# First-step results split on VectorE between S's steps, and the last norm's statistics between later rounds of the search

## The chip, the core and the metric

The kernel runs on one core of a Trainium2 chip. The metric is the device time of one execution, in microseconds; the median of three executions of the kernel before is 3901.39 us.

## The reference

The graph has N = 2708 nodes with D = 512 features. Layer 0 is a graph attention layer with eight heads; layer 1, which the change touches, mixes three diffusions over two steps:

```python
S = S + jnp.eye(n)
Rf = S / jnp.clip(S.sum(axis=1, keepdims=True), 1e-12)
Rb = S / jnp.clip(S.sum(axis=0), 1e-12)[:, None]
Xf, Xb, Xa = (X, X, X)
Z = jnp.zeros_like(X)
for s in range(2):
    A = _adj_from_feats(Xa, W1, W2, W3)
    Xf = Rf @ Xf
    Xb = Rb @ Xb
    Xa = A @ Xa
    Z = Z + (Xf @ U1[s] + Xb @ U2[s] + Xa @ U3[s])
Y = X + Z
return (Y - Y.mean(-1)) / jnp.sqrt(Y.var(-1) + 1e-5) * gamma + beta
```

`_adj_from_feats` builds logits between all nodes, keeps of each row the largest softmax entries until 0.9 of the mass is reached, and takes the softmax over what is kept. Both layers are added to their input.

## The kernel before

The 2708 rows are 22 tiles of 128 (the last has 20). Layer 0 comes first and leaves `va_d` (the input of layer 1), a copy of it split into high and low parts (`vhl_d`), and S itself in memory (`s_d`). Then the second half runs, which the change is about.

**Rounds.** Each of the two steps handles the tiles in eleven pairs, one pair a round. In a round, VectorE searches the thresholds of the next pair (`search`), while TensorE uses the pair that has been found: `attended` transposes its kept weights (L1092), ScalarE copies the transposes out (`at`, L1096), and TensorE multiplies them with the values (L1111) in twelve chunks, six a tile. `mixed` then multiplies by U1, U2 and U3 (L1147). At a round's start TensorE makes the logits of the pair after next (L514), ScalarE copies them out (`p`, L516).

**The search.** `search` works in a first part (`rounds`: two rounds of the search in the first step and four in the second, each with two passes over the rows, L621), `choose`, and a last part, `finish`, which writes `keep` (L797 and after). Between `choose` and `finish` the function `late` is called: it records all of the round's work on TensorE, ScalarE and SP. On VectorE, what `late` records therefore stands between `choose` and `finish`. `keep` has two buffers, so `finish` waits until TensorE has transposed the pair before.

**Fills.** For the pair after next, ScalarE takes the exponentials and twelve looks (L546) over the logits, with thresholds `nth` (L566) that GpSimd works out from their sums in some ten small operations (L558 to L566). These are paced between the chunks of `attended`, so in ScalarE's order they stand between the `at` copies.

**S's products.** The products with S don't depend on the attention. The class `Products` cuts them into steps that are taken between the chunks as `others`. For each of six groups of up to four tiles (`quad`), 22 steps `product` (8 matmuls each, L982) make S times X, with operands `hl` and `s_r` that SP loads three deep (L972, L974). A step `scaled` then scales a tile on ScalarE by rows and by columns (`xe`, L989) and GpSimd's queue stores both to `xfb_d` (L990). The second step needs the products of these results, again as high and low parts: `split` loads a tile back on GpSimd's queue (L1019), splits it on GpSimd by four operations with 4097 (L1020 to L1023), and stores it to `fhl_d` or `bhl_d` (L1024). The buffers `split_hl` are two. In the steps `turned` (L999) TensorE uses these parts, and `stored` copies the results out (`xe`, L1005) and stores them to `xt_d` on GpSimd's queue (L1006). The first step takes 26 of these steps ahead of its rounds, 26 more in the round g = −1, and then 17 or 18 a round. `split(7)` is called at the start of the rounds after the first.

**The last norm.** In the second step, the finished rows `yo` of a round are normed in the next one. `normed` is called ahead of that round's search: statistics on VectorE (L143, L144), the inverse root on GpSimd (L145, L146), and a load of the residual on SP's queue (L1176). What it returns applies them (L1179, L1180) in the search's second round, `it == 1`.

**Order.** TensorE, ScalarE, VectorE and SP keep the order in which the program records their instructions; GpSimd's instructions are placed by the scheduler by its estimate of when each is ready. Every engine works through its own order and waits where it must. A DMA is issued in the order of the engine that issues it, and a DMA's wait holds up what that engine has behind it.

Of the kernel before, what the change touches and what calls it, by code (L numbers as in the profile page):

```python
# [9 lines left out]
F32 = mybir.dt.float32  # L10
BF16 = mybir.dt.bfloat16
I32 = mybir.dt.int32
# [3 lines left out]
OP = mybir.AluOpType  # L16
# [8 lines left out]
P = 128  # L25
# [28 lines left out]
def kernel(  # L54
# [19 lines left out]
    nc = tc.nc  # L74
    N, D = x.shape
# [6 lines left out]
    rows = [min(P, N - i * P) for i in range(NT)]  # L82
    cols = [slice(i * P, i * P + rows[i]) for i in range(NT)]
# [115 lines left out]
    with ExitStack() as l0:  # L199
# [13 lines left out]
        with tc.tile_pool(name="l0w", bufs=1) as wp, tc.tile_pool(name="l0p", bufs=2) as pp, \  # L213
# [376 lines left out]
    def search(lg, looked, early, late):  # L590

        (wide, small, _), grp, ps_, tot, thr, s = lg.pools, lg.grp, lg.p, lg.tot, lg.thr, lg.s
        v = nc.vector
        nx = NEXT[s]
# [53 lines left out]
        def rounds(n, aim_at=None):  # L650
            for it in range(n):
                v.tensor_tensor(d, ends[:, 1, 0:2], ends[:, 0, 0:2], op=OP.subtract)
                v.tensor_scalar(d[:, 1], d[:, 1], -1e-12, None, op0=OP.min)
                v.reciprocal(fr, d[:, 1])
                v.tensor_mul(fr, fr, ends[:, 0, 1])
                v.tensor_scalar(fr, fr, -0.95, -0.05, op0=OP.max, op1=OP.min)
                v.tensor_mul(fr, fr, d[:, 0])
                v.tensor_tensor(cur[:, 0], ends[:, 0, 0], fr, op=OP.subtract)
                v.tensor_mul(th, cur[:, 0], cur[:, 0])
                v.tensor_mul(th, th, th)  # L660
                if it in (aim_at or ()):
                    v.tensor_copy(fr, g0)
                    aim(g0, th)
                    v.tensor_tensor(fr, fr, g0, op=OP.subtract)
                    v.tensor_tensor(ends[:, :, 1], ends[:, :, 1], fr.unsqueeze(1).to_broadcast([P, 2, G]), op=OP.add)
                if it == 1 and begun:
                    begun.pop()()
                for i, pr in tiles:
                    mass(i, pr, th[:pr, i:i + 1], cur[:pr, 2, i:i + 1])
                v.tensor_tensor(fr, lg.top, cur[:, 2], op=OP.subtract)  # L670
                v.reciprocal(fr, fr)
                v.tensor_tensor(cur[:, 1], fr, g0, op=OP.subtract)
                v.scalar_tensor_tensor(side, cur[:, 1].unsqueeze(1).to_broadcast([P, 2, G]), 0.0, sides,
                                       op0=OP.is_ge, op1=OP.not_equal)
                v.copy_predicated(ends, side.unsqueeze(2).to_broadcast([P, 2, 3, G]),
                                  cur.unsqueeze(1).to_broadcast([P, 2, 3, G]))
                if it == 0 and aim_at is not None:
                    begun.append(early())

        begun = []  # L680
        rounds(ROUNDS[s], (0,) if s else ())
# [221 lines left out]
    with ExitStack() as st:  # L903
# [38 lines left out]
        class Products:  # L942
# [3 lines left out]


            def __init__(self):
                self.steps, self.ready, self.splits, self.split_at = [], {}, [], 0
# [35 lines left out]
            def scaled(self, t, j):  # L985
                pr = rows[t]
                for i, inv in enumerate((rinv, cinv)):
                    x = work.tile([P, D], F32, name="xe")
                    nc.scalar.activation(x[:pr], self.half[j][:pr], AF.Copy, scale=inv[:pr, t:t + 1])  # L989
                    nc.gpsimd.dma_start(out=xfb_d[i, cols[t], :], in_=x[:pr])  # L990
                    self.splits.append((i, t))

            def turned(self, quad, i, c):
                while (i, c) not in self.splits[:self.split_at]:
                    self.split(1)
                hl, s_r, w = self.operands((fhl_d, bhl_d)[i], quad, c)
                for k in range(KD):
                    for h in range(2):
                        nc.tensor.matmul(self.half[k][:, :w], lhsT=hl[:, h, k * P:(k + 1) * P], rhs=s_r[:, :w],  # L999
                                         start=(c == 0 and h == 0), stop=(c == NT - 1 and h == 1))  # L1000

            def stored(self, quad, q, i, k):
                w = len(quad) * P
                x = work.tile([P, D], F32, name="xe")
                nc.scalar.copy(x[:, :w], self.half[k][:, :w])  # L1005
                nc.gpsimd.dma_start(out=xt_d[q, i, :, k, :w], in_=x[:, :w])  # L1006

            def split(self, n):


                for i, t in self.splits[self.split_at:self.split_at + n]:
                    self.split_at += 1
                    pr = rows[t]
                    hl = parts.tile([P, 2, D], F32, name="split_hl")
                    x4 = parts.tile([P, D], F32, name="x4097", bufs=1)
                    if pr < P:
                        nc.gpsimd.memset(hl, 0.0)
                    high, x = hl[:pr, 0], hl[:pr, 1]
                    nc.gpsimd.dma_start(out=x, in_=xfb_d[i, cols[t], :])  # L1019
                    nc.gpsimd.tensor_scalar(x4[:pr], x, 4097.0, None, op0=OP.mult)  # L1020
                    nc.gpsimd.tensor_tensor(high, x4[:pr], x, op=OP.subtract)
                    nc.gpsimd.tensor_tensor(high, x4[:pr], high, op=OP.subtract)
                    nc.gpsimd.tensor_tensor(x, x, high, op=OP.subtract)  # L1023
                    nc.gpsimd.dma_start(out=(fhl_d, bhl_d)[i][t * P:(t + 1) * P], in_=hl)  # L1024

        S = Products()

# [143 lines left out]
        def normed(t, y):  # L1171

            pr = rows[t]
            mean, rs = moments(small, y[:pr], pr)
            xb = work.tile([P, D], F32, name="xw")
            nc.sync.dma_start(out=xb[:pr], in_=xb_d[cols[t], :])  # L1176

            def rest():
                nc.vector.scalar_tensor_tensor(y[:pr], y[:pr], mean, g_b[:pr], op0=OP.subtract, op1=OP.mult)  # L1179
                nc.vector.scalar_tensor_tensor(y[:pr], y[:pr], rs, xb[:pr], op0=OP.mult, op1=OP.add)  # L1180
                nc.gpsimd.dma_start(out=out[cols[t], :], in_=y[:pr])  # L1181

            return rest
# [61 lines left out]
        with tc.manual_schedule(engines={PE, ACT, DVE, SP}):  # L1245
            rest_of_first = []
            for s in range(STEPS):
# [37 lines left out]
                for g in range(-1, NP):  # L1285
# [4 lines left out]
                    if g + 3 < NP:  # L1290
                        lg.append(logits(g + 3))
                        lg[g + 3].queries()
                    if not s and g > 0:
                        S.split(7)
                    norms = [normed(t, y) for t, y in done] if s else []
                    done = []
                    if g < 0:
                        n = BEGUN - first if s else NT + 2 * G
# [60 lines left out]
                    if g + 1 < NP:  # L1359
                        ready = search(lg[g + 1], g >= 0, early, late)  # L1360
                    else:
                        if not s:

                            load_keys(1, 0, known * P)
                            ranks = Ranks()
                            others.insert(min(8, len(others)), lambda: ranks.sums(0, known))
                        for rest in norms:
                            rest()
                        late()
                        if not s:  # L1370
                            ranks.counted(0, known)
# [33 lines left out]
```

## Time and profile before

| | us |
|---|---|
| median of three runs | 3901.39 (3899.46 to 3902.29) |
| span of the profiled execution | 3908.7 |
| TensorE (PE) busy | 3388.9 (87%) |
| VectorE (DVE) busy | 2678.3 (69%) |
| ScalarE (ACT) busy | 1503.9 (38%) |
| GpSimd (POOL) busy | 1216.0 (31%) |
| first step's rounds, from the first transpose to the end of the last pair | 1302 to 2463 |
| second step's rounds, between the first and the last reciprocal of the kept mass that bound ten of them | 2710.8 to 3827.2 |

The profile is of one execution, taken with the hardware profiler. An engine is busy while it executes; waiting and issuing DMAs don't count, and TensorE's ends are modelled. A row of a group of instructions gives the line, the engine, the operation and its tiles, then the busy time and the mean duration, then the idle time of the engine before it and what ended that. "PE a L1111 <- ACT at L1096" in the view of waits says that the matmul of line 1111 waited for ScalarE's copy of line 1096. The clock is the share of TensorE's full clock that was granted.

### The profile page before, as it was taken

Reading aid. Unit: us, or ns where it says so; the run is one execution under the profiler, and the core shown is the slowest. Engines: PE = TensorE matmul, PEld = TensorE weight load, DVE = VectorE, ACT = ScalarE, POOL = GpSimd, SP = SyncE. Lnnn points to the kernel's source line nnn. Section 1 sums busy time; section 2 is a strip of 40 time slices with the busy share of each in tenths; the row PEclk is TensorE's granted clock in tenths of the full one; section 3 lists DMA queues with packets and bytes.
Section 4 is the critical chain, followed back from the end, with each engine's and each line's share of the span. In section 5 each row is a group of like instructions: output and inputs, shape, how many; then the busy total and the mean of one; then the engine's idle time right before and its main releaser. Section 6 shows DMA issues by size and latency. Waiting matters only on the chain. (4 is left out here: it accounts for less than half of the span.)

```text
span 3908.7 us, 35336 instructions
## 1 busy us (share of the span) xinstructions
PE 3388.9 (87%) x11058; PEld 1755.4 (45%) x11058; DVE 2678.3 (69%) x4727; ACT 1503.9 (38%) x2275; POOL 1216.0 (31%) x1447
## 2 busy tenths in 40 slices
PE   8998999999765596898789999976999699998787
PEld 4333333334444353554445555534555355554442
DVE  4687898899852443455544454369799978988992
ACT  2343211111124354544455661135555444545510
POOL 4115142243315717263641221122221232123211
PEclk9999999999878798999899999988999899999898
DMA  3475433323169555564554445565555355565441
GB/s 111 158 265 201 143 101 116 99 83 110 38 208 329 187 169 174 176 211 159 199 186 157 167 156 186 165 215 178 183 174 194 106 200 166 181 210 174 138 163 58
DMA packets 287348, 644.27 MB, mean 165 GB/s; under 512 B 37852, under 2 KB 86638, under 8 KB 284132
## 3 DMA queue, kind: packets, MB, share of 16 engines
q1 hardware_dynamic: 256488, 539.64, 42.3%
q0 software_dynamic: 30608, 101.84, 7.1%
q8 instruction: 89, 1.46, 0.2%
q14 instruction: 163, 1.34, 0.1%
HBM read 518.78 MB, written 122.57 MB: 164 GB/s over the span
## 5 line engine op out<-in xcount | busy, mean ns | idle before, releaser
L1111 PE MATMUL a<-va,at 128*128 128x512 f32 (+2 forms) x1936 | 910.6, 610 | 73.6 <-ACT at L1096 73.3
L426 PE MATMUL po<-e,fw 128*65 128x512 f32 (+4 forms) x2112 | 839.6, 553 | 33.7 <-DVE e L424 21.1
L424 DVE SCALAR_TENSOR_TENSOR e<-r_b,kk,a_c 128x512 f32<-128x512 f32 (+4 forms) x1056 | 752.2, 740 | 72.9 <-PE po L426 22.4
L546 ACT ACTIVATE junk_a<-p,nth 128x2708 uint8<-128x2708 f32 (+1 forms) x240 | 612.8, 2553 | 192.3 <-POOL nth L566 188.5
L999 PE MATMUL q<-s_r,hl 128*128 128x512 f32 (+1 forms) x2112 | 550.4, 409 | 75.3 <-ACT xe L1005 38.0
L1111 PEld LDWEIGHTS a<-va,at 128*128 128x128 f32 (+2 forms) x1936 | 344.5, 190 | 455.1 <-issue 354.3
L1147 PE MATMUL a<-u_k,v_t 128*128 128x512 f32 (+1 forms) x1056 | 491.2, 608 | 58.3 <-POOL v_t L1056 25.2
L426 PEld LDWEIGHTS po<-e,fw 128*65 128x65 f32 (+1 forms) x2112 | 287.1, 140 | 546.9 <-issue 269.5
L999 PEld LDWEIGHTS q<-s_r,hl 128*128 128x128 f32 x2112 | 381.3, 193 | 239.2 <-issue 92.6
L797 DVE SCALAR_TENSOR_TENSOR keep<-p,th 128x2708 f32<-128x2708 f32 (+1 forms) x44 | 134.5, 3056 | 466.0 <-PE t L1092 464.8
L621 DVE SCALAR_TENSOR_TENSOR junk<-p,th 128x2708 bf16<-128x2708 f32 (+1 forms) x132 | 414.6, 3141 | 4.0
L982 PE MATMUL q<-hl,s_r 128*128 128x512 f32 x968 | 275.8, 435 | 77.6 <-DMA s_r<-s_d 58.8
L1096 ACT COPY at<-t 128x512 f32<-128x512 f32 (+3 forms) x308 | 139.6, 474 | 496.1 <-PE t L1092 495.8
L1147 PEld LDWEIGHTS a<-u_k,v_t 128*128 128x128 f32 (+1 forms) x1056 | 191.1, 189 | 300.1 <-issue 206.2
L982 PEld LDWEIGHTS q<-hl,s_r 128*128 128x128 f32 x968 | 188.8, 199 | 158.6 <-issue 67.6
L514 PE MATMUL t<-keys,q_t 128*128 128x452 f32 x528 | 159.6, 426 | 97.0 <-ACT p L516 76.1
L799 DVE MAX8 vn<-keep 128x8 f32<-128x2708 f32 (+1 forms) x66 | 196.8, 2981 | 2.3
L541 DVE TENSOR_REDUCE nmx<-p 128x1 f32<-128x2708 f32 (+1 forms) x44 | 129.6, 2968 | 87.5 <-ACT p L516 87.4
L1056 POOL TENSOR_TENSOR v_t<-v_t,scales 128x1024 f32<-128x1024 f32 (+1 forms) x33 | 117.0, 3555 | 226.6 <-ACT v_t L1044 183.3
L1092 PE MATMUL t<-ident,keep 128*128 128x128 f32 (+1 forms) x968 | 148.3, 276 | 40.1 <-DVE keep L749 19.2
L516 ACT COPY p<-t 128x452 f32<-128x452 f32 (+2 forms) x264 | 130.9, 540 | 130.8 <-PE t L514 81.9
L408 ACT ACTIVATE s_c<-a_c 128x512 fp32r<-128x512 f32 (+3 forms) x132 | 76.2, 577 | 251.1 <-DMA a_c<-in_adj_t_dram 123.3
(313 smaller groups left out, 3536.4 us busy)
## 6 DMA issues: line engine op xcount, KB each, us to landing
s_r<-s_d SPq DMA_DIRECT2D x330, 256.0 KB
hl<-vhl_d SPq DMA_DIRECT2D x132, 512.0 KB
u_k<-in_L_gnn_U_dram SPq DMA_DIRECT2D x264, 256.0 KB
hl<-fhl_d SPq DMA_DIRECT2D x132, 512.0 KB
hl<-bhl_d SPq DMA_DIRECT2D x132, 512.0 KB
arow<-in_adj_dram SPq DMA_DIRECT2D x21, 1354.0 KB
s_d<-s_c SPq DMA_DIRECT2D x88, 256.0 KB
a_c<-in_adj_t_dram SPq DMA_DIRECT2D x84, 256.0 KB
```

The costliest lines, as they stand in the source:

```text
L424: nc.vector.scalar_tensor_tensor(e[:pr, :cw], r_b[:pr, i, :cw], kk[:pr, t, hd:hd + 1], a_c[t][:pr, :cw], op0=OP.max, op1=OP.mult)
L426: nc.tensor.matmul(po[i][:, :cw], lhsT=fw[:pr, t, hd, :], rhs=e[:pr, :cw], start=(t == 0), stop=(t == NT - 1))
L514: nc.tensor.matmul(pl[:, :c1 - c0], lhsT=q[:, i], rhs=self.keys[:, c0:c1], start=(i == 0), stop=(i == 1))
L546: nc.scalar.activation(junk[:pr], self.p[i][:pr], func, **kw)
L621: v.scalar_tensor_tensor(junk_b[:pr], ps_[i][:pr], th, ps_[i][:pr], op0=OP.is_ge, op1=OP.mult, accum_out=dst)
L799: v.max(vs, keep[i][:pr])
L982: nc.tensor.matmul(self.half[j], lhsT=s_r[:, j * P:(j + 1) * P], rhs=hl[:, h], start=(c == 0 and h == 0), stop=(c == NT - 1 and h == 1))
L999: nc.tensor.matmul(self.half[k][:, :w], lhsT=hl[:, h, k * P:(k + 1) * P], rhs=s_r[:, :w], start=(c == 0 and h == 0), stop=(c == NT - 1 and ...
L1092: nc.tensor.transpose(pt[:rows[c], j, :pr], keep[i][:pr, cols[c]], ident[:pr, :pr])
L1096: nc.scalar.copy(at[:r, j0:j1, :pr], pt[:r, j0:j1, :pr])
L1111: nc.tensor.matmul(pa[:pr], lhsT=at[:rows[c], j, :pr], rhs=va[:rows[c], c, :], start=(c == 0), stop=(c == NT - 1))
L1147: nc.tensor.matmul(pz[i][:rows[t]], lhsT=v_t[:, k, i * P:i * P + rows[t]], rhs=u_k, start=(n == 0 and k == 0), stop=(n == 2 and k == KD - 1))
```

## The change

Three parts of `Products` change. `split` no longer computes on GpSimd: it loads a tile on SP's queue, and at its next call masks the low bits away and subtracts on VectorE, and stores on GpSimd's queue. It is called one by one after S's steps 1 to 8 of each of the first step's rounds (`splitting`), instead of seven at a round's start. The stores of `scaled` and `stored` are issued by ScalarE. Besides, the last norm's statistics and its load are recorded in the search's third round, and their application in the fourth. All else is the same, TensorE's order too.

```diff
-                if it == 1 and begun:
-                    begun.pop()()
+                if it > 1 and begun:
+                    begun.pop(0)()
...
-                    begun.append(early())
+                    begun.extend(early())
...
-                    nc.gpsimd.dma_start(out=xfb_d[i, cols[t], :], in_=x[:pr])
+                    nc.scalar.dma_start(out=xfb_d[i, cols[t], :], in_=x[:pr])
...
-                nc.gpsimd.dma_start(out=xt_d[q, i, :, k, :w], in_=x[:, :w])
+                nc.scalar.dma_start(out=xt_d[q, i, :, k, :w], in_=x[:, :w])
...
-            def split(self, n):
+            def split(self):
...
-                for i, t in self.splits[self.split_at:self.split_at + n]:
+                for i, t, hl in self.taken:
+                    pr = rows[t]
+                    nc.vector.tensor_scalar(hl[:pr, 0].bitcast(I32), hl[:pr, 1].bitcast(I32), -4096, None,
+                                            op0=OP.bitwise_and)
+                    nc.vector.tensor_tensor(hl[:pr, 1], hl[:pr, 1], hl[:pr, 0], op=OP.subtract)
+                    nc.gpsimd.dma_start(out=(fhl_d, bhl_d)[i][t * P:(t + 1) * P], in_=hl)
                     self.split_at += 1
+                self.taken = []
+                if self.split_at < len(self.splits):
+                    i, t = self.splits[self.split_at]
                     pr = rows[t]
                     hl = parts.tile([P, 2, D], F32, name="split_hl")
-                    x4 = parts.tile([P, D], F32, name="x4097", bufs=1)
                     if pr < P:
                         nc.gpsimd.memset(hl, 0.0)
-                    high, x = hl[:pr, 0], hl[:pr, 1]
-                    nc.gpsimd.dma_start(out=x, in_=xfb_d[i, cols[t], :])
-                    nc.gpsimd.tensor_scalar(x4[:pr], x, 4097.0, None, op0=OP.mult)
-                    nc.gpsimd.tensor_tensor(high, x4[:pr], x, op=OP.subtract)
-                    nc.gpsimd.tensor_tensor(high, x4[:pr], high, op=OP.subtract)
-                    nc.gpsimd.tensor_tensor(x, x, high, op=OP.subtract)
-                    nc.gpsimd.dma_start(out=(fhl_d, bhl_d)[i][t * P:(t + 1) * P], in_=hl)
+                    nc.sync.dma_start(out=hl[:pr, 1], in_=xfb_d[i, cols[t], :])
+                    self.taken.append((i, t, hl))
...
+            def splitting(self, steps, n):
...
+                return [(lambda step=step: both(step)) if 0 < k < n else step for k, step in enumerate(steps)]
...
-                    if not s and g > 0:
-                        S.split(7)
-                    norms = [normed(t, y) for t, y in done] if s else []
+                    norms = done if s else []
...
-                    others = S.take(n)
+                    others = S.take(n) if s or g < 0 else S.splitting(S.take(n), 9)
...
-                        return lambda: [rest() for rest in norms]
+                        held = []
+                        return [lambda: held.extend(normed(*x) for x in norms), lambda: [rest() for rest in held]]
...
-                        for rest in norms:
+                        held = [normed(*x) for x in norms]
+                        for rest in held:
                             rest()
```

In VectorE's order the 44 splits stand between `choose` and `finish` of seven searches, by 7, 8, 8, 8, 7, 2 and 4. In SP's order each of the 44 loads stands behind the operands of the S step after which it is called. In GpSimd's order, in the first five of these rounds, the stores of five splits stand ahead of the operations that end in `nth`.

More of the change, by code (lines that the diff above doesn't have):

```diff
@@ L948, in __init__ @@
             def __init__(self):
-                self.steps, self.ready, self.splits, self.split_at = [], {}, [], 0
+                self.steps, self.ready, self.splits, self.split_at, self.taken = [], {}, [], 0, []
                 self.at = 0
@@ L994, in turned @@
                 while (i, c) not in self.splits[:self.split_at]:
-                    self.split(1)
+                    self.split()
                 hl, s_r, w = self.operands((fhl_d, bhl_d)[i], quad, c)
@@ L1005, in stored, with both @@
                 nc.scalar.copy(x[:, :w], self.half[k][:, :w])
-                nc.gpsimd.dma_start(out=xt_d[q, i, :, k, :w], in_=x[:, :w])
-            def split(self, n):
-                for i, t in self.splits[self.split_at:self.split_at + n]:
+                nc.scalar.dma_start(out=xt_d[q, i, :, k, :w], in_=x[:, :w])
[6 more added lines that the diff above has]
+                    nc.gpsimd.dma_start(out=(fhl_d, bhl_d)[i][t * P:(t + 1) * P], in_=hl)
                     self.split_at += 1
+                self.taken = []
+                if self.split_at < len(self.splits):
+                    i, t = self.splits[self.split_at]
                     pr = rows[t]
                     hl = parts.tile([P, 2, D], F32, name="split_hl")
-                    x4 = parts.tile([P, D], F32, name="x4097", bufs=1)
                     if pr < P:
                         nc.gpsimd.memset(hl, 0.0)
-                    high, x = hl[:pr, 0], hl[:pr, 1]
-                    nc.gpsimd.dma_start(out=x, in_=xfb_d[i, cols[t], :])
-                    nc.gpsimd.tensor_scalar(x4[:pr], x, 4097.0, None, op0=OP.mult)
-                    nc.gpsimd.tensor_tensor(high, x4[:pr], x, op=OP.subtract)
-                    nc.gpsimd.tensor_tensor(high, x4[:pr], high, op=OP.subtract)
-                    nc.gpsimd.tensor_tensor(x, x, high, op=OP.subtract)
-                    nc.gpsimd.dma_start(out=(fhl_d, bhl_d)[i][t * P:(t + 1) * P], in_=hl)
+                    nc.sync.dma_start(out=hl[:pr, 1], in_=xfb_d[i, cols[t], :])
+                    self.taken.append((i, t, hl))
+            def splitting(self, steps, n):
+                def both(step):
+                    step()
+                    self.split()
+                return [(lambda step=step: both(step)) if 0 < k < n else step for k, step in enumerate(steps)]
         S = Products()
```

## The prediction

> **What bounds the kernel now.** I read the page's engine shares first, then busy time by stretches of the first step's rounds, then who waited for whom inside them, then the timeline of single rounds. TensorE is busy 87% of the span, so the question is where its other 13% sits. The first step's rounds divide at 2055 us: the results of the first product are split into high and low parts on GpSimd until then, and no longer after it. The view by stretches (length, PE, PEld, DVE, ACT and POOL busy, clock, DMA share, GB/s):
>
> ```profile
> 1302.00:2055.00 753.00, 630.32 (x2072) 354.17 (x2072) 370.35 (x682) 369.24 (x460) 370.92 (x416) 0.92 0.53 180
> 2055.00:2463.00 408.00, 398.48 (x1378) 230.44 (x1378) 192.65 (x412) 185.20 (x236) 70.87 (x114) 1.00 0.51 168
> ```
>
> Six rounds with splits leave TensorE idle for 122.7 us and have POOL half busy; the nearly four rounds after leave 9.5 us. DVE and ACT have the same load per round in both. So POOL's work is the suspect. Who waited for whom, on TensorE between 1302 and 2055 us (total, times, longest):
>
> ```profile
> PE a L1111 <- ACT at L1096: 57.3, 14, 23.5
> PE a L1147 <- POOL v_t L1056: 25.2, 3, 18.1
> PE q L982 <- ACT xe L989: 18.7, 4, 9.1
> ```
>
> And on ScalarE between 1200 and 2055 us:
>
> ```profile
> ACT junk_a L546 <- POOL nth L566: 92.1, 7, 30.6
> ACT xe L989 <- DMA xfb_d<-xe: 42.9, 10, 11.1
> ```
>
> On TensorE after 2055 us the first row is 1.5 us and the two behind it are gone. The timeline shows the link: POOL works through split after split, and the thresholds `nth` come behind them.
>
> ```profile
> 1352.62 1.49 POOL L1020 TENSOR_SCALAR x<-split_hl 128x512 f32<-128x512 f32 x1 [2.31 <-DMA split_hl<-xfb_d]
> ...
> 1356.87 1.26 POOL L1023 TENSOR_TENSOR split_hl<-split_hl 128x512 f32<-128x512 f32 x1
> 1358.42 0.61 POOL L1024 DMA_DIRECT2D bhl_d<-split_hl  x1 [0.30 <-POOL split_hl L1023]
> 1359.07 0.74 POOL L559 TENSOR_TENSOR x<-half,powers 128x2 f32<-128x2 f32 x1
> ```
>
> The same moment on ScalarE:
>
> ```profile
> 1363.72 2.55 ACT L546 ACTIVATE junk_a<-p,nth 128x2708 uint8<-128x2708 f32 x1 [30.58 <-POOL nth L566]
> ```
>
> ScalarE's next `at` copy stands behind that look in its order, and TensorE waits 23.5 us for it at 1367.5. In the second step VectorE is the tighter engine: from 2710.8 to 3827.2 us (1116.4 us) it is busy 989.0, much as TensorE's 990.0. Its one avoidable wait there is for `yo`:
>
> ```profile
> DVE ln_st L143 <- POOL yo L1163: 93.3, 11, 64.2
> ```
>
> 64.2 us of it is the last norm of all, at the kernel's end; 26.4 us are in three rounds (13.1, 10.1, 3.2).
>
> **What the Trainium skill says.** "GPSIMD Engine Reference", section 4.1, sends elementwise work to VectorE, GpSimd being about twice as slow with two inputs; the trace agrees: POOL's four split operations take 1.49, 1.27, 1.27 and 1.27 us, VectorE's mask of the same shape (L178) 0.42. "VectorE: DVE Perf Modes", on the TRN2 errata, gives a float32 add of N elements (N+151)/0.96 ns, 0.69 us at 512; L239 shows 0.684. "DMA: Bandwidth & Descriptors", "Issuing engines are not separate DMA queues", says that issuing from another engine saves only issue time; so I book no bandwidth for it. "TensorE: Matmul & The Clock Gate", Part 1, ties the clock to how busy TensorE is; the stretches' 0.92 against 1.00 agree.
>
> **The change part by part.**
>
> *Splits leave POOL.* Removed per split: four operations, 1.87+1.56+1.27+1.40 = 6.1 us by their means, and a load issue of 0.59; 44 splits, 268+26 us. The stores of `xe` (92) leave POOL too, 51 us of issue. What this is worth is read from TensorE's idle time. If the six rounds were idle in the share of the rounds after (9.5 of 408), they would take 630.3/0.977 = 645 us: −108. A clock nearer 1.00 could make the busy time itself shorter: 304 ns a matmul record against 289, at most −31; the mix of matmuls differs, so I take −15. Before 1302, TensorE waits 22.2 us at 1293.7 for ScalarE, which had waited 24.4 us for `nth` and 11.1 for an `xfb` store; eight evacuations on two buffers stay there, some 9 us: −13.
>
> *Splits enter VectorE.* Two operations, 0.42+0.69 = 1.11 us, 44 times: 49 us, in seven rounds' `late`, ahead of `finish` in VectorE's order. There VectorE waits anyway for TensorE's transposes to free `keep`: 30 to 50 us in each of these rounds (41.6 until 1770.3, 49.5 until 1893.2). On the path: 0.
>
> *Loads enter SP's queue, two buffers.* This is the new wait. Load n needs the store of split n−2 landed, which needs VectorE to have come past its search; behind the waiting load stand the operands `hl` and `s_r` of S's next step, three deep, for which TensorE waits. I clock it from TensorE's first transpose of a round, called T. VectorE comes free at T+13 (2177 against 2164). Landing times by the DMA view, KB and us:
>
> ```profile
> vhl_d<-split_hl POOLq DMA_DIRECT2D x22, 512.0 KB, 2.9
> fhl_d<-split_hl POOLq DMA_DIRECT2D x22, 512.0 KB, 4.8
> ...
> split_hl<-xfb_d POOLq DMA_DIRECT2D x42, 256.0 KB, 3.5
> ```
>
> One turn of a buffer is 3.5 (load) + 1.1 (VectorE) + 0.6 (POOL's issue) + 4.8 = 10.0 us, two splits a turn. The split left over from the round before goes at T+13, is stored at T+19, and lets load 2 go; loads 4, 6 and 8 follow at about T+29, T+38 and T+48, the odd ones a microsecond behind. TensorE needs S's step k at T+4+5.9k while it does one a chunk (3.9 us of attention and 2 of S), and two in 7.5 us later: steps 7 and 9 at T+39 and T+49, whose operands land at T+41.5 and T+51. So some 5 us a round are lost in the five rounds that split seven or eight, +23; the ends are 0, where the store lands in 2.9 us as `vhl_d`'s does, and 12 a round, where it takes 3 us longer.
>
> *Stores of the splits stay on POOL.* In its order five stand ahead of the points of the pair after next. The fifth split is done at T+33, so `nth` comes at T+38 instead of T+29.6 (2193.5 in the round from 2163.9). ScalarE's look waits, and behind it the copy `at` that TensorE needs at T+41.6; look, `xa` and copy end at T+42: 1 to 3 us a round, +10 in all.
>
> *Stores issued by ScalarE.* 92 at some 0.4 us, as SP's rows have (0.32 to 0.43), behind ScalarE's own copy: 37 us on an engine that is idle 40 us and more a round. The waits for `xfb` and `xt` stores (42.9 and 11.0 us) shrink in return. ScalarE's copies are on TensorE's path, so this can be −10 to +15; I take 0.
>
> *Last norm.* The same 18 pairs of statistics and applications, two rounds of the search later; its loads don't move in SP's queue. VectorE starts a search 26.4 us earlier in all. At the third round, some 28 us after the search's start, `yo` (at most 13.1 after it) is there, so no wait follows. TensorE is nearly as full, so half is worth time: −13 (0 to −26).
>
> Sum: −108 −15 −13 +23 +10 −13 = −116. On the profiled span, 3908.7 to 3793. The timed runs have 3901.4 as median, 0.2% less; from there 3785.
>
> **Rivals.**
> 1. *The splits are freed but wait in line* (small gain). SP's loads are bound to VectorE and to landings, and turns of 13 us instead of 10 cost 12 us more a round, 60 more in all, with `nth` behind them 3 us a round later: about −40, 3860. For it: these are SP's first waits on VectorE in these rounds; against: SP's slack of three steps.
> 2. *Slower.* The same mechanism where it decides: the load at the head of SP's queue holds S's operands. The recovered idle time is 23 us a round in six rounds. It is lost from the point where VectorE comes free at T+31 rather than T+13, or a turn takes 15 us: four turns then end at T+73 against TensorE's T+49. A turn of 18 us would cost 36 us a round, 165 in 4.6 rounds, and ScalarE's copies behind `nth` another 40; against the 149 that the sum has without its new waits (116+23+10) that is +56, 3957. Against it: VectorE's T+13 holds in each round that TensorE bounds.
> 3. *It does not act.* If ScalarE's own load (59 us a round) rather than `nth` delayed `at`, only the waits for `xe` and `v_t` (49 us, half of it worth time) and for the norms go, −38, and +33 of new waits stand against them: 3896. Against it: after 2055 us ScalarE has the same load and TensorE waits 1.5 us.
>
> **How the numbers follow.** The forecast: 0.72, own range 3745 to 3830. Rival 1: 0.18. Rival 2: 0.06. Rival 3: 0.04. The best case, all idle time and clock recovered and no new wait, is −108−31−22−26 = −187, 3714. The range drops the ends of the first and all of rivals 2 and 3: 3735 to 3862. A measurement here can tell about 0.2% (8 us) from no change: faster 0.91, within it 0.03, slower 0.06.
>
> **What would show it.** Right: TensorE's waits for `at` between the first round and the end of the splits fall from 57 to under 25 us, the ones for `v_t` go; each of these rounds takes 104 to 112 us. SP shows waits of a `split_hl` load for VectorE or a store, and TensorE short waits for `s_r` behind them. VectorE's wait at L143 is left with the last one, of 64 us. Wrong: POOL's `nth` still late, now behind the stores; TensorE waiting over 10 us a round for `hl` or `s_r`; or VectorE's `keep` starting after TensorE's transposes.

## The result and the profile after

The changed kernel takes 3887.38 us (median of four executions, 3882.66 to 3888.83) against 3901.84 of the kernel before on the same chip: a ratio of 0.9958, 95% interval 0.9941 to 0.9975. That is 16 us faster. The prediction was 3785 us and its range ended at 3862, so the direction was right and the size was not.

The profiled executions (3908.7 us before, 3880.9 after) show that the change did two opposite things. Take as marks the starts of the rounds, the moment at which VectorE has the pair's `rden` (L898 before, L899 after). Lines from `split` on are 11 higher after: L1092, L1096, L1111, L1147 are now L1103, L1107, L1122, L1158.

| | before | after | difference |
|---|---|---|---|
| up to the first round of the second step | 2710.8 | 2632.1 | −78.7 |
| from there to the last round (second step) | 1116.4 | 1170.6 | +54.2 |
| last round and the norm at the end | 81.5 | 78.2 | −3.3 |

**The first step** went the way that the prediction described, for less: −78.7 us, where the terms of the splits in the prediction add to −103. The view by stretches (length; PE, PEld, DVE, ACT and POOL busy; clock, DMA share, GB/s) of the six rounds after the first, and of the second step, before:

```profile
1417.60:2144.50 726.90, 627.44 (x2068) 352.06 (x2066) 352.31 (x673) 369.55 (x460) 328.75 (x384) 0.94 0.54 180
...
2710.80:3827.20 1116.40, 990.01 (x3361) 562.21 (x3361) 989.00 (x1817) 538.47 (x644) 266.78 (x275) 0.95 0.50 167
```

and after:

```profile
1378.70:2062.70 684.00, 622.92 (x2067) 352.77 (x2065) 351.16 (x746) 372.30 (x460) 133.67 (x225) 0.97 0.59 201
...
2632.10:3802.70 1170.60, 1004.94 (x3361) 569.07 (x3361) 987.41 (x1817) 541.45 (x644) 307.42 (x241) 0.93 0.48 159
```

In the first row of each, POOL falls from 329 to 134 us and TensorE's idle time (length less PE busy) from 99.5 to 61.1 us. In the second row TensorE, VectorE and ScalarE have as many instructions as before, and yet the stretch is 54 us longer: 39 us of it are idle time of TensorE, 15 its busy time, at a clock of 0.93 instead of 0.95. GpSimd has fewer instructions, and is busy 41 us longer (the last section takes this up). Who waited for whom on TensorE in those six rounds, after:

```profile
PE a L1122 <- ACT at L1107: 17.1, 13, 5.1
PE q L983 <- DMA s_r<-s_d: 16.2, 11, 3.6
PE q L983 <- ACT xe L990: 9.3, 4, 6.2
```

The waits for `v_t` (25.2) are gone, those for `at` have halved from 33.8, and short ones for `s_r` are new: each what the prediction named. But the six rounds take 106 to 124 us each, where it had 104 to 112.

**The second step** holds what it did not name. Its waits after, as total, times and longest:

```profile
POOL ln_rs L145 <- DVE ln_mv L144: 145.2, 9, 30.3
...
POOL out_dram L1192 <- DVE yo L1191: 40.3, 18, 4.2
...
ACT junk_a L546 <- POOL nth L566: 135.0, 9, 23.6
...
PE a L1122 <- ACT at L1107: 51.5, 17, 17.5
...
DVE keep L798 <- PE t L1103: 61.7, 8, 15.2
```

Before, the same five were 36.6, 129.4, 73.4, 13.7 and 0.7 us. Read from the top it is a ring: GpSimd waits for VectorE's statistics, the thresholds `nth` come late, ScalarE's looks wait for them and its `at` copies behind the looks, TensorE waits for `at`, and VectorE waits for TensorE's transposes before it may write `keep`. The timeline of GpSimd in one round (start, duration; the idle time before and its end in brackets) shows the head of the ring:

```profile
3367.24 0.23 POOL L145 TENSOR_SCALAR ln_rs<-ln_mv 128x1 f32<-128x1 f32 x1 [17.69 <-DVE ln_mv L144]
3367.55 0.58 POOL L146 TENSOR_TENSOR ln_rs<-ln_rs,nhalf 128x1 f32<-128x1 f32 x1
3368.11 2.83 POOL L145 TENSOR_SCALAR ln_rs<-ln_mv 128x1 f32<-128x1 f32 x1
3371.03 3.35 POOL L146 TENSOR_TENSOR ln_rs<-ln_rs,nhalf 128x1 f32<-128x1 f32 x1
3374.35 0.70 POOL L559 TENSOR_TENSOR x<-half,powers 128x2 f32<-128x2 f32 x1
3378.56 0.67 POOL L1192 DMA_DIRECT2D out_dram<-yo  x1 [3.51 <-DVE yo L1191]
...
3391.55 0.25 POOL L566 TENSOR_SCALAR nth<-th_a 128x6 f32<-128x6 f32 x1
```

The norm's small operations (L145, L146) and its stores (L1192) are GpSimd's, and in GpSimd's order they stand ahead of the points of the pair after next, L558 to L566. `nth` is there 61.0 us after the round's start at 3330.8. The same in the kernel before, where the store waits for an application that VectorE makes in the search's second round; `nth` ends at 3429.9, 44.5 us after the round's start at 3385.4:

```profile
3413.58 0.64 POOL L1181 DMA_DIRECT2D out_dram<-yo  x1 [19.34 <-DVE yo L1180]
...
3419.91 1.46 POOL L558 TENSOR_TENSOR x<-tot,powers 128x2 f32<-128x2 f32 x1 [1.60 <-ACT p L553]
...
3426.89 3.04 POOL L566 TENSOR_SCALAR nth<-th_a 128x6 f32<-128x6 f32 x1
```

Here the store is not what comes last: behind it GpSimd still waits 1.60 us for the exponentials that ScalarE makes for the pair after next (L553). Over the second step before there are nine such waits, 15.6 us; after the change one is left, of 0.2 us. So before, the norm was done when the exponentials came; after, the exponentials are done when the norm comes.

ScalarE and TensorE at the end of the chain, after:

```profile
3391.83 2.55 ACT L546 ACTIVATE junk_a<-p,nth 128x2708 uint8<-128x2708 f32 x1 [19.01 <-POOL nth L566]
...
3397.67 2.93 PE L1122 MATMUL a<-va,at 128*128 128x512 f32 x3 [10.40 <-ACT at L1107]
```

### The profile page after: what moved, and what is told of

Same layout as the page of the kernel before. It is cut to its first block, busy times and chain, and to the rows that moved or that the text cites. A ratio compares the mean times of both kernels' runs of the same rounds, so it can differ in the third digit from the quotient of the medians.

```text
span 3880.9 us, 35319 instructions
## 1 busy us (share of the span) xinstructions
PE 3394.0 (87%) x11058; PEld 1755.9 (45%) x11058; DVE 2669.8 (69%) x4815; ACT 1511.9 (39%) x2275; POOL 929.9 (24%) x1135
## 5 line engine op out<-in xcount | busy, mean ns | idle before, releaser
L1122 PE MATMUL a<-va,at 128*128 128x512 f32 (+2 forms) x1936 | 910.9, 610 | 70.9 <-ACT at L1107 70.7
L1122 PEld LDWEIGHTS a<-va,at 128*128 128x128 f32 (+2 forms) x1936 | 345.2, 191 | 453.3 <-issue 353.4
L1158 PE MATMUL a<-u_k,v_t 128*128 128x512 f32 (+1 forms) x1056 | 487.3, 604 | 32.5 <-ACT xa L1130 18.7
L1107 ACT COPY at<-t 128x512 f32<-128x512 f32 (+3 forms) x308 | 140.4, 477 | 518.7 <-PE t L1103 513.0
L1158 PEld LDWEIGHTS a<-u_k,v_t 128*128 128x128 f32 (+1 forms) x1056 | 190.7, 188 | 270.5 <-issue 207.7
L1067 POOL TENSOR_TENSOR v_t<-v_t,scales 128x1024 f32<-128x1024 f32 (+1 forms) x33 | 98.0, 2982 | 425.2 <-ACT v_t L1055 343.4
L1103 PE MATMUL t<-ident,keep 128*128 128x128 f32 (+1 forms) x968 | 149.6, 277 | 28.5 <-DVEq L882 16.6
```

The lines of the kernel that those rows point to most:

```text
L1103: nc.tensor.transpose(pt[:rows[c], j, :pr], keep[i][:pr, cols[c]], ident[:pr, :pr])
L1107: nc.scalar.copy(at[:r, j0:j1, :pr], pt[:r, j0:j1, :pr])
L1122: nc.tensor.matmul(pa[:pr], lhsT=at[:rows[c], j, :pr], rhs=va[:rows[c], c, :], start=(c == 0), stop=(c == NT - 1))
L1158: nc.tensor.matmul(pz[i][:rows[t]], lhsT=v_t[:, k, i * P:i * P + rows[t]], rhs=u_k, start=(n == 0 and k == 0), stop=(n == 2 and k == KD - 1))
```

## The experiments

Theory A: the second step's loss comes from the norm, through GpSimd's order. Rival B: it comes from the stores that ScalarE now issues, or from a lower clock (0.93 against 0.95). Each ratio below is to the kernel before, with its 95% interval; microseconds from ratios are on 3902 us.

### The norm undone, and the norm alone

The changed kernel with the norm's part taken back, and the kernel before with that part alone:

```diff
-                if it > 1 and begun:
-                    begun.pop(0)()
+                if it == 1 and begun:
+                    begun.pop()()
...
-                    norms = done if s else []
+                    norms = [normed(t, y) for t, y in done] if s else []
```

> The changed kernel with only its norm part undone: the last norm's statistics stand again ahead of the search and the application in the search's second round; splits and stores stay as changed. Theory A (the second step's loss of 54 us comes from the norm: GpSimd waits for VectorE's later statistics and application with the thresholds of the pair after next behind it) expects about 3887-54 = 3833 us (3825 to 3845), the second step back at some 1116 us, ScalarE's wait for nth there near 73 us. Rival B (the loss comes from ScalarE issuing the xt stores, or from a lower clock) expects 3887 within 8 us, second step still near 1170 us.

> The kernel before with the norm part alone. Theory A expects it slower by the second step's loss less the few us won at the end: 3902+54-3 = about 3950 us (3935 to 3960), with GpSimd waiting at L145 some 145 us in all. Rival B expects no change, 3894 to 3905.

Undone: 3848.57 us, 0.9867 (0.9851 to 0.9884), so the norm's part costs the changed kernel 0.9958−0.9867, about 36 us. Alone: 3945.74 us, 1.0115 (1.0096 to 1.0134), 45 us slower than before. Theory A's direction holds twice and rival B's "no change" falls. The undone version misses A's 3825 to 3845 by 4 us: its second step is 1129.5 us, 13 longer than before, so not all of the 54 us is the norm's. That remainder stays in part open; the section on the stores has what is known of it. The lower clock comes with the norm's part: with that part alone, which leaves TensorE's order as it was, it falls to 0.93 too.

### One round sooner, off GpSimd's queue, and the store alone moved

Three versions of the changed kernel move the last thing that GpSimd waits for. The first runs both pieces one round of the search sooner:

```diff
-                if it > 1 and begun:
+                if it > 0 and begun:
```

The second takes the statistics ahead of the search again, and has the store of the output issued by SyncE, recorded behind the attention's operands; the third moves only the store:

```diff
-                nc.gpsimd.dma_start(out=out[cols[t], :], in_=y[:pr])
+                return lambda: nc.sync.dma_start(out=out[cols[t], :], in_=y[:pr])
...
                             xa, _ = attended(s, grp, keep, rden, fills, others, lambda: None)
+                            for store in stores:
+                                store()
```

> The changed kernel with the norm's two pieces one round of the search earlier each: statistics in the second round, application in the third. Theory A expects about half of the loss back, as GpSimd's wait shrinks by one round (some 9 us of 17 a pair): 3855 to 3872 us, GpSimd's wait at L145 at 50 to 80 us instead of 145. Rival B expects 3887 within 8 us.

> The changed kernel with the statistics ahead of the search again, the application left late (third round), and the store of the output issued by SyncE behind the attention's operands, so that nothing late of the norm is in GpSimd's queue. Theory A (it is the queue and not the lateness) expects the loss back and a little more, since the store no longer holds GpSimd either (19 us in one round of the kernel before): 3810 to 3835 us. If lateness itself costs (the buffer of yo, VectorE's order), it stays above 3865. Rival B expects 3887 within 8 us.

> The changed kernel with only the store of the output taken out of GpSimd's queue (SyncE issues it behind the attention's operands); statistics stay in the third round of the search. GpSimd waits 145 us at ln_rs and 42 us at the store in the changed kernel's second step. If ln_rs, which stands first, is what holds nth up, little comes back: 3875 to 3887. If the store is the one, 3840 to 3855.

They take 3845.65 us (0.9861, 0.9845 to 0.9878), 3842.46 us (0.9852, 0.9836 to 0.9868) and 3849.6 us (0.9854, 0.9836 to 0.9873): alike, and each some 40 us better than the changed kernel. Two expectations were off: one round sooner brings back all that undoing the norm does, not half of it, and off GpSimd's queue misses its 3810 to 3835 by 7 us, so that freeing GpSimd from the store won nothing further. Of the two cases set up for the store alone, the second came true, although GpSimd's longer wait is at L145. A long wait at L145 only says where GpSimd arrives first; `nth` follows the last thing that it waits for, and that was the store behind an application in the fourth round. With the store gone the last is the statistics in the third. The two versions whose last thing is in the third round also have the same waits. One round sooner:

```profile
ACT junk_a L546 <- POOL nth L566: 98.0, 9, 18.3
...
DVE keep L798 <- PE t L1103: 24.7, 7, 9.4
```

Only the store moved:

```profile
ACT junk_a L546 <- POOL nth L566: 99.9, 9, 18.3
...
DVE keep L798 <- PE t L1103: 24.8, 6, 10.7
```

So the norm's part is a trade on VectorE: it saves the waits for `yo` (28.9 us in the second step before) and pays with waits for `keep`. The search round of the norm's last thing ahead of `nth` sets ScalarE's wait for `nth`. VectorE's waits in the second step are given as a pair (for `keep` + for `yo`); the last row is the last version of the experiments:

| kernel | norm's last thing, search round | ScalarE's wait for `nth` | VectorE's waits | second step |
|---|---|---|---|---|
| before | application, 2nd | 73.4 | 0.7 + 28.9 | 1116.4 |
| norm alone | application, 4th | 134.2 | 63.2 + 0 | 1162.7 |
| norm undone | application, 2nd | 72.3 | 0.7 + 33.6 | 1129.5 |
| off GpSimd's queue | statistics, ahead | 77.6 | 2.0 + 38.1 | 1132.5 |
| one round sooner | application, 3rd | 98.0 | 24.7 + 0 | 1133.6 |
| only the store moved | statistics, 3rd | 99.9 | 24.8 + 0 | 1135.8 |
| changed | application, 4th | 135.0 | 61.7 + 0 | 1170.6 |
| last version below | statistics, 2nd | 74.4 | 13.2 + 0 | 1118.1 |

The first two rows have the splits and stores of the kernel before; the last has the stores on GpSimd and a third buffer for `xe`. The fourth round costs 46 us against the second on the kernel before, and 35 us or more against all others on the changed one. Between the third round and a norm ahead of the search the second step hardly differs (1132.5 to 1135.8): one wait takes the other's place.

### Stores issued by ScalarE

> The kernel before with only the stores of xe moved to ScalarE; splits and norm as before. If the splits themselves (6.1 us each) hold nth up, this wins little: 51 us of 345 us leave GpSimd and ScalarE waits less for xfb (47.5 us), 3880 to 3895. Rival: GpSimd's blocking on stores that wait for ScalarE (55.6 us at L990) is the main thing; then it wins most of the 55 us, 3845 to 3865.

> The kernel before with only the 44 xfb stores issued by ScalarE. Both kinds of stores together gave +15 us (+11 to +22). If it is the xfb stores (first step: the split's loads behind them wait up to 24.5 us on GpSimd, TensorE's first-round wait for s_r grows from 21.9 to 31.4), +8 to +15: 3910 to 3920. If it is the xt stores, 3898 to 3906.

> The kernel before with only the 48 xt stores issued by ScalarE. If the cost lies here (second step 1126 us instead of 1117), 3910 to 3918; else 3898 to 3906.

> The version with the norm off GpSimd's queue (3842 us), with the 92 stores of xe issued by GpSimd again. The prediction has their move at 0 (-10 to +15): 3842 within 8 us. Rival: the move is what costs the second step some 13 us there (ScalarE issues 44 xt stores among its copies), then this is faster, 3825 to 3835. Other rival: the stores behind other work on GpSimd make ScalarE wait for xe again (47.5 us before), then slower, 3855 or more.

The edit, whole and by halves, and the reverse of it on the version with the norm off GpSimd's queue:

```diff
-                    nc.gpsimd.dma_start(out=xfb_d[i, cols[t], :], in_=x[:pr])
+                    nc.scalar.dma_start(out=xfb_d[i, cols[t], :], in_=x[:pr])
...
-                nc.gpsimd.dma_start(out=xt_d[q, i, :, k, :w], in_=x[:, :w])
+                nc.scalar.dma_start(out=xt_d[q, i, :, k, :w], in_=x[:, :w])
```

Alone on the kernel before, ScalarE's stores cost time: 3918.25 us, 1.0043 (1.0029 to 1.0057), 17 us; both theories of that run, which had a gain, were wrong. By halves: the `xfb` stores do nothing, 1.0002 (0.999 to 1.0014); the `xt` stores cost 1.0024 (1.0011 to 1.0037), 9 us, and the second step, in which 32 of the 48 lie, takes 1132.9 us. The halves add to less than the whole, but the intervals allow it. Back on GpSimd in the version with the norm off its queue: 3838.82 us, 0.9832 (0.9819 to 0.9845), 8 us less than with ScalarE, but the two intervals overlap. So this part is a loss on the kernel before. How the `xt` stores cause it stays open: no wait of TensorE, ScalarE or VectorE in the second step is longer by more than 7 us than in the second profile of the kernel before (next run), but for one of 14.8 us for `yo` on ScalarE that another row has less of; VectorE's waits there grow by 6.5 (`rden`) and 4.5 us (`yo`), PE busy by 9.

> The kernel before once more, for a second profile: whether its second step takes 1116 us again (then the versions with the splits moved, 1130 us there, lose some 13 us to something that the change does) or some 1125 to 1130 us (then that difference is the spread between executions).

A second profile of the kernel before has its second step at 1117.7 us, and the version with only the `xfb` stores moved has 1117.6. So the 1126.3 us of all stores and the 1132.9 of the `xt` stores on ScalarE hardly come from the spread between executions alone, though with one profile each their size is uncertain. On the versions with the splits on VectorE the second step doesn't show it: with the norm off GpSimd's queue it takes 1132.5 us with the stores on ScalarE and 1133.4 with them back on GpSimd. The split part alone (next), stores on GpSimd, has 1124.8. So the 13 us left over above are not explained by the stores' issuer alone. With the norm's statistics and application moved so that no wait for `yo` is left, they go (1118.1 us, last version below).

### The splits alone, and without their loads and operations

> The kernel before with the split part alone: masks and differences on VectorE, loads on SyncE; stores of xe on GpSimd and norm as before. The prediction's terms for this part are -108-15-13+23+10 = -103, 3798. From the runs so far (-52 for splits and ScalarE's stores together, the stores +7 to +15 of it) it should give -60 to -67, 3835 to 3843. If the two parts need each other, less than that.

> The split part alone, without the split: no load of the results and no operation, only one load at the start, whose rows are stored 44 times in place of the high and low parts (so later products with them compute other values; the searches don't depend on them). SyncE, VectorE and the turn of two buffers are then out of it. The prediction's terms without its new waits are -108-15-13 = -136, which would be 3769. If the splits still cost what the prediction has for waits (33 us), this is 33 us faster than the split part alone (3835): about 3802. If the missing gain was never theirs (idle time on TensorE from p, xe and the first operands), 3820 to 3835, with TensorE still idle over 45 us in the six rounds after the first (69.6 in the split part alone).

The split part alone (stores and norm as before) takes 3834.78 us, 0.9821 (0.9807 to 0.9836): −70 us. It is the better part of the change by itself; with ScalarE's stores added it is the version with the norm undone (0.9867, +18 us), with the norm's part the changed kernel (0.9958, +36 us). The other run leaves the split out, and puts this in place of `split`'s body:

```diff
-                for i, t, hl in self.taken:
...
+                if self.split_at < len(self.splits):
+                    i, t = self.splits[self.split_at]
+                    if not self.taken:
+                        self.taken.append(parts.tile([P, 2, D], F32, name="split_hl"))
+                        nc.sync.dma_start(out=self.taken[0], in_=vhl_d[:P])
+                    nc.gpsimd.dma_start(out=(fhl_d, bhl_d)[i][t * P:(t + 1) * P], in_=self.taken[0])
+                    self.split_at += 1
```

It takes 3798.69 us, 0.9725 (0.9708 to 0.9741): −107 us, and by the ratios 37 less than the split part alone. As its stores wait for no result, GpSimd issues all 44 by 1339 us, in the first round, so the six rounds behind it have no split's load, operation or store. These six rounds, by the view of stretches:

```profile
1371.80:2024.60 652.80, 613.49 (x2070) 347.58 (x2068) 310.90 (x672) 369.06 (x460) 123.35 (x214) 0.98 0.50 168
```

and those of the split part alone, with TensorE's longest row of waits there:

```profile
1369.30:2064.40 695.10, 625.55 (x2067) 352.79 (x2065) 351.22 (x746) 370.16 (x460) 147.96 (x253) 0.96 0.58 198
```

```profile
PE q L983 <- DMA s_r<-s_d: 26.0, 9, 8.4
```

Without the split the row for `s_r` is gone and the waits for `at` hardly differ, 14.6 against 15.3 us. TensorE's idle time is 39.3 us instead of 69.6, its busy time 12 us less at a clock of 0.98 instead of 0.96. So the split on its new engines still costs some 37 us; in these rounds 26 are TensorE's waits for S's operands, 12 its busy time. As the run takes out the loads, VectorE's two operations and the stores' traffic together (the DMA share falls from 0.58 to 0.50), how much each has is not shown; the waits for `s_r` fit the loads in SyncE's queue. And 39 us of idle time are not the splits' at all: 14.6 for `at`, 11.6 for `xe`, 10.2 for `p` and the rest in crumbs.

### Loads on GpSimd, and a third buffer

Both on the version with the norm off GpSimd's queue (0.9852):

```diff
-                    nc.sync.dma_start(out=hl[:pr, 1], in_=xfb_d[i, cols[t], :])
+                    nc.gpsimd.dma_start(out=hl[:pr, 1], in_=xfb_d[i, cols[t], :])
```

> The version with the norm off GpSimd's queue (3842 us), with the loads of the splits issued by GpSimd instead of SyncE: nothing that waits for a split's store stands ahead of S's operands any more. If SyncE's wait for the two buffers costs what the prediction has (23 us; TensorE's waits for s_r there are 54.2, of which 28.0 is one at the first round's start), they fall to some 30 us and the time to about 3820 (3815 to 3832). Rival: the waits for s_r come from elsewhere (the operands' own landing, TensorE taking steps in twos) or move into GpSimd's queue ahead of nth; then the time stays within 8 us of 3842 or rises.

It changes nothing in all: 3850.95 us, 0.9855 (0.9841 to 0.9868). Inside, the wait has moved. TensorE, 1194 to 2060 us, loads on SyncE:

```profile
PE q L983 <- DMA s_r<-s_d: 54.2, 24, 28.0
...
PE a L1122 <- ACT at L1107: 18.5, 15, 5.5
```

and loads on GpSimd:

```profile
PE a L1122 <- ACT at L1107: 41.2, 16, 8.8
PE q L983 <- DMA s_r<-s_d: 40.1, 12, 30.3
```

The one long wait at the first round's start apart, `s_r` falls from 26 to 10 us, and `at` rises by 23, as now the points stand behind the split's loads: ScalarE's wait for `nth` in this stretch rises from 35.1 to 63.0 us. The load has to wait in somebody's queue, and both queues carry something TensorE needs.

```diff
-                    x = work.tile([P, D], F32, name="xe")
+                    x = work.tile([P, D], F32, name="xe", bufs=3)
```

> The version with the norm off GpSimd's queue (3842 us), with three buffers for xe instead of two. In the eight evacuations ahead of the first round ScalarE waits about 12.5 us for xfb stores and TensorE 19.2 us for the logits' copy behind them; with a third buffer that should fall by 4 to 8 us: 3832 to 3840. Rival: the round's start is set by something else (VectorE's thresholds), then no change.

3832.55 us, 0.9817 (0.9804 to 0.9831), by the ratios 14 us less, more than the 4 to 8 expected. ScalarE's wait for `xfb` stores falls from 20.2 to 10.3 us, TensorE's for the logits' copies at the first round from 19.2 to 15.8. These 3.4 us are all that the trace shows on TensorE; where the rest would come from is not shown.

### Versions that beat both kernels

> Splits on VectorE as changed, norm off GpSimd's queue, three buffers for xe, stores of xe on GpSimd. If the gains of the third buffer (-13 us against 3842) and of the stores left on GpSimd (-7) add, 3820 to 3830; if both are the same wait for a free xe, 3832 as with the third buffer alone.

> Splits on VectorE; xe stores on GpSimd, three xe buffers; the norm's statistics in the second round of the search, its application in the third, the store of the output on SyncE, so that the last thing GpSimd waits for ahead of the thresholds is in the second round, and VectorE no longer waits for yo (28.9 us in the second step of the kernel before). If VectorE's wait is worth half of its time there, as the prediction has it, some 13 us better than 3832: 3815 to 3825. If GpSimd's wait eats it, 3828 to 3836.

The first takes 3832.32 us, 0.9806 (0.9788 to 0.9825): the third buffer and GpSimd's stores don't add. The second changes only the norm against it: statistics in the search's second round, application in the third, the store on SyncE. It takes 3815.91 us, 0.9763 (0.9749 to 0.9778), 17 us less again and 76 less than the changed kernel by the ratios. In its second step VectorE's waits are the smallest of all (13.2 for `keep`, no row for `yo`), and the stretch is back at 1118.1 us, from 1130.1:

```profile
2615.70:3733.80 1118.10, 992.32 (x3361) 563.50 (x3361) 1000.52 (x1817) 539.22 (x644) 305.67 (x255) 0.95 0.50 166
```

## Why the prediction was wrong, by its own steps

**"Last norm", −13, "so no wait follows": the step that failed.** Measured +36 (+45 on the kernel before): of the 100 us between the predicted sum and the result, half. The step followed VectorE's queue and SyncE's. Of the moved code it counted the statistics, the applications and the loads; it left out what the same two functions issue on GpSimd, the small operations L145 and L146 and the two stores of the output, and so never asked what stands behind them. Behind them stands `nth`, the one thing that the first half of the prediction was about. The trace of before had a sign of it: GpSimd waited 19.34 us for VectorE's `yo` at the output's store, right ahead of L559, and its wait behind that for the exponentials was 1.60 us, which leaves some 2 us of room for a later norm (an estimate from this one round). What the step said of VectorE itself held: it no longer waits for `yo`. The saving itself was of the right size: where the norm's last thing ahead of `nth` stays in the second round, it is 17 us.

**"Splits leave POOL" −108, clock −15, before 1302 us −13: right mechanism, −107 measured for the three instead of −136.** That is the run without loads and operations. The term that was too large is −108: it took the idle share of the rounds after 2055 us (9.5 of 408 us) for all rounds. Those rounds have 1.5 us of waits for `at` and 3.3 for `xe`; the six rounds with splits keep 14.6 and 11.6 even when no split is computed. The first round's term was too large too: TensorE's wait for the logits' copies fell from 22.2 to 17.1 us in that run (19.9 in the changed kernel), not by 13. The clock's term held without the splits' waits (PE busy 613.5 against 627.4), not with them (622.9).

**"Loads enter SP's queue, two buffers" +23, "Stores of the splits stay on POOL" +10: +37 measured together.** The sum was nearly right, its division was not, and that is luck. `s_r` waits are 26.0 us in the split part alone, near the +23. `at` waits hardly differ with and without the split, so the +10 is not there; in its place TensorE's busy time is 12 us longer, at a lower clock.

**"Splits enter VectorE", 0 on the path: held.** The new subtraction took 0.693 us a time, as priced from the Trainium skill, "VectorE: DVE Perf Modes", TRN2 errata; the mask took 0.427, as the trace of before had it for L178. GpSimd's 1.27 us for an operation with two inputs are to be set beside these 0.693, not beside the mask as the prediction does: a factor of 1.8. VectorE is busy 351 us in the six rounds as before (352), which the prediction had not said: some 41 us of splits came in, and VectorE's other operations became 42 us shorter (see the last section).

**"Stores issued by ScalarE", 0 (−10 to +15): +17 and +18 measured.** That is just past the bad end of its bounds; taking the stores back on another version won 8 us, with overlapping intervals. ScalarE's 42.9 us of waits for `xfb` did shrink, to about half, but no time was won by it.

Taken one on top of the other, the parts measure −70 for the splits, +18 for the stores and +36 for the norm; that they add to −16 is no further evidence, since each is the step from one version to the next. Against the predicted −116 the norm is off by 49 us, the splits by 33 and the stores by 18. Of the rivals, the first came nearest to the time but names another cause: the splits' waits are about of the size forecast. None put a loss into the second step.

## What to carry to other kernels

When a step is moved, list what it issues on every engine, the two-operation helper and the store at its end too, and for each ask what stands behind it in that engine's order; an engine that is idle most of the time, as GpSimd is here, can still hold up the result when it waits at one instruction with another engine's work behind it. A wait's length tells where an engine arrived early, not what holds the result up: ask which wait ends last. A stretch without the trouble is a fair measure of the gain only if it has the same kinds of work, so compare its small rows too before taking its idle share.

## What was not expected of the hardware

GpSimd's small operations stretch to the length of VectorE's passes. In the timeline above, L145 and L146 on one column take 2.83 and 3.35 us where they overlap VectorE's two search passes, which run from 3367.86 to 3370.87 and from 3370.91 to 3373.95, and 0.23 and 0.58 us just before them. Over the second step L145 takes 1531 ns on average, against 223 in the kernel before, and L146 1962 against 577: standing directly ahead of the passes costs GpSimd 5 us more a round.

It works the other way too. In the six rounds with splits before, VectorE's operation L866 on one column takes 688 ns on average, and 161 after (L867), L803 on eight columns 587 and 234 (L804). In all, VectorE's operations other than the splits take 352.3 us before, 309.8 after, and 310.9 in the run that leaves the split out. So while GpSimd computed the splits, they cost VectorE some 42 us, as much as they take on VectorE itself.

That L145 and L146 end within 0.1 and 0.5 us of the ends of the passes suggests that the two engines share something; no run took this apart.
